# Raw x in tiles of its own, low-rank products in two steps, and the fold in four row groups, in a two-layer attention kernel

## Chip, cores and metric

The kernel runs on one core of one Trainium2 chip. The metric is the device time of one execution in microseconds, as the median of several runs.

## What is computed

The input is an image of 48 x 48 positions with 768 channels, that is 2304 tokens. Two layers follow each other. Each takes its input, normalises it over groups of 24 channels, applies self-attention with 12 heads of 64 channels and relative-position terms, projects, and adds the result to its input. Cut to what matters:

```python
def _gn(v, G=32, eps=1e-5):                 # over all positions and 24 channels
    g = v.reshape(B_, H_, W_, G, C_ // G)
    m = jnp.mean(g, axis=(1, 2, 4), keepdims=True)
    s = jnp.var(g, axis=(1, 2, 4), keepdims=True)
    return ((g - m) / jnp.sqrt(s + eps)).reshape(v.shape)

def _L0_conv_ref(x, qkv_w, qkv_b, FacTu_w, q_facts_w, v_facts_w, FacTv_w, ...):
    qkv = x @ qkv_w + qkv_b
    u = x @ FacTu_w                          # rank 16
    new_q = u @ q_facts_w @ FacTv_w
    new_v = u @ v_facts_w @ FacTv_w
    qkv = qkv.at[..., :C].add(new_q).at[..., 2 * C:].add(new_v)
    ...                                      # q, k, v by heads
    attn = jnp.einsum('bqc,bkc->bqk', q * scale, k)
    attn = ...                               # + rel_h over rows, + rel_w over columns
    out = jax.nn.softmax(attn, axis=-1) @ v
    return out @ proj_w + proj_b

x = x + _L0_conv_ref(_gn(x), ...)
x = x + _L1_conv_ref(_gn(x), ...)            # the same without the low-rank terms
```

The kernel doesn't compute u for every token. It multiplies the three small factors into a 768 x 768 update, and adds this to the weights of Q and V. That addition is the *fold*.

## The kernel before

Tokens are tiled in six blocks (`NQB`) of 384 (`QB`), each with three tiles of 128 (`TPB`); channels are six tiles of 128 (`CT`). Everything works on x transposed, with channels on the partitions: `xT`, one SBUF tile of 128 x 6 x 2304.

**The start of layer 0** is `load_transposed`. SyncE's queue issues six loads of x into tiles `xt` of a pool of their own (L166). Then `weights.begin()` issues the small operands: the low-rank factors `fu` (FacTu), `facts` (the two 16 x 16 factors) and `out` (FacTv, called `fv` in the trace) on ScalarE's queue, the biases and the relative-position tables on SyncE's, and GpSimd (POOL) spreads the tables with L273. `weights.load(0)` and `load(1)` issue the weights of K and Q of the first half of the heads (L299). For each of the 36 pairs of block and channel tile TensorE makes three transposes into a PSUM tile `psx` (L177, three buffers), ScalarE copies it to `xT` (L178), and VectorE takes the statistics from there (L179). After each block, GpSimd's queue stores the raw block to DRAM for the later residual addition (L180, `f_res`). Ahead of block 4 comes `low_rank()`: for each half of the channels three transposes of `fu` (L285), a copy to `fuT` (L286), and for each of the two factors a product (L290, `psl`, 16 rows of result) and a copy to `low` (L293), with two PSUM buffers from the pool `ps_f`.

**The normalisation** (`group_norm`) aggregates the statistics (L187), sums over groups and brings them back to channels with tiny matmuls on TensorE, takes a square root on ScalarE, and returns `normalise(b)`, which rewrites `xT` in place (L226), six operations to a block.

**The projections** (`project`) go through two halves of the heads, and in each through K, Q and V. K and Q come from `head_rows`: 18 PSUM tiles `ps` (pool `ps_mm`, four buffers), each the sum of six matmuls in fp32 (L432), which the hardware's records show as two passes each; VectorE adds the bias (L443), and the result is split into a rounded part (L328, ScalarE) and a difference (L329, VectorE), which GpSimd's queue stores (L369). Q also feeds the relative-position products (L376, `psr`, `psc`). V is 18 tiles `psv` (L461). Before Q and before V, `take` calls `fold`: six matmuls of 16 rows (L320, `psf`, two buffers in `ps_f`), and VectorE adds each into the weights (L324).

**The rest**: attention of six pairs of heads over the stored q, k, v and relative-position products (TensorE under one line, L705), then `out_project` (L874), which also takes the statistics for layer 1, stores its raw input, and leaves `xT` filled.

The order on each engine is a scheduler's, made ahead of time; what is wrapped in `in_order` keeps its place in the program. Each engine takes its instructions in that order, and so does each DMA queue. A second path of the program (`shifted`), which a test on the softmax denominators would start, isn't run with this data.

Of the kernel before, what the change touches and what calls it, by code (L numbers as in the profile page):

```python
# [17 lines left out]
P = 128  # L18
C = 768
# [51 lines left out]
def compute(ctx: ExitStack, tc: tile.TileContext, x, layers, out, run, bad):  # L71
# [72 lines left out]
    if not shifted:  # L144
        places = const.tile([P, 2, P], F32R, tag="places", name="places")
        for i in range(4):
            nc.gpsimd.dma_start(
                places[ts(i, 2 * KG)].bitcast(F32), hot.rearrange("k (u n) -> k u n", u=2)
            )
# [8 lines left out]
    def load_transposed(xT, res, weights):  # L158

        with tc.tile_pool(name="xin", bufs=NQB) as xin, tc.tile_pool(  # L160
            name="ps_x", bufs=3, space=PSUM
        ) as ps_x:
            xts = []
            for b in range(NQB):
                xt = xin.tile([P, TPB, C], F32, tag="xt", name=f"xt_{b}")
                nc.sync.dma_start(xt, x[ts(b, QB), :].rearrange("(j p) c -> p j c", p=P))  # L166
                xts.append(xt)
            weights.begin()
            weights.load(0)
            weights.load(1)  # L170
            for b, xt in enumerate(xts):
                if b == 4:
                    weights.low_rank()
                for t in range(CT):
                    ps = ps_x.tile([P, QB], F32, tag="ps", name=f"psx_{b}_{t}")
                    for j in range(TPB):
                        in_order(nc.tensor.transpose(ps[:, ts(j, P)], xt[:, j, ts(t, P)], ident))  # L177
                    nc.scalar.copy(xT[:, t, ts(b, QB)], ps)  # L178
                    nc.vector.bn_stats(stats[:, t, b, :], xT[:, t, ts(b, QB)])  # L179
                nc.gpsimd.dma_start(res[b], xT[:, :, ts(b, QB)])  # L180

    def group_norm(xT, gn):
# [41 lines left out]
        def normalise(b):  # L224
            for t in range(CT):
                nc.vector.tensor_scalar(  # L226
                    xT[:, t, ts(b, QB)], xT[:, t, ts(b, QB)], mean[:, t : t + 1],
                    rstd[:, t : t + 1], ALU.subtract, ALU.mult,
                )
# [3 lines left out]
    class Weights:  # L233
# [13 lines left out]
        def begin(self):  # L247
            one, ly = self.one, self.ly
            if ly.lora is not None:
                u_w, q_f, v_f, o_w = ly.lora  # L250
                self.fu = one.tile([P, CT, RANK], F32, tag="fu", name="fu")
                nc.scalar.dma_start(self.fu, u_w.rearrange("(t p) r -> p t r", p=P))
                self.facts = one.tile([RANK, 2, RANK], F32, tag="facts", name="facts")
                nc.scalar.dma_start(self.facts[:, 0, :], q_f)
                nc.scalar.dma_start(self.facts[:, 1, :], v_f)
                self.out = one.tile([RANK, C], F32, tag="fv", name="fv")
                nc.scalar.dma_start(self.out, o_w)
            self.bt = one.tile([P, 3 * CT], F32, tag="bt", name="bt")
            nc.sync.dma_start(self.bt, ly.qkv_bt)
            self.vb = one.tile([P, C], F32, tag="vb", name="vb")  # L260
            nc.sync.dma_start(self.vb, ly.v_b.to_broadcast((P, C)))

            self.tables = []
            for a, src in enumerate((ly.relh_t, ly.relw_t)):
                flat = one.tile([P, REL], F32, tag=f"flat{a}", name=f"flat{a}")
                tab = one.tile([P, REL, 2], F32, tag=f"tab{a}", name=f"tab{a}")
                nc.gpsimd.memset(tab, 0.0)
                for par in range(2):  # L270
                    half_rows = ts(par, HD)
                    nc.sync.dma_start(flat[half_rows, :], src)
                    nc.gpsimd.tensor_copy(tab[half_rows, :, par], flat[half_rows, :])  # L273
                self.tables.append(tab.rearrange("p k r -> p (k r)"))
        def low_rank(self):

            if self.ly.lora is None:
                return
            fuT = self.one.tile([RANK, C], F32, tag="fuT", name="fuT")
            self.low = self.one.tile([RANK, 2, C], F32, tag="low", name="low")  # L280
            for half in range(2):
                cols = ts(half, HP * P)
                ps = self.ps.tile([P, HP * P], F32, tag="f", name=f"psu_{half}")[0:RANK]
                for t in range(HP):
                    in_order(nc.tensor.transpose(ps[:, ts(t, P)], self.fu[:, half * HP + t, :], ident))  # L285
                nc.vector.tensor_copy(fuT[:, cols], ps)  # L286
                for i in range(2):
                    ps = self.ps.tile([P, HP * P], F32, tag="f", name=f"psl_{half}_{i}")
                    ps = ps[0:RANK]
                    in_order(nc.tensor.matmul(  # L290
                        ps, lhsT=self.facts[:, i, :], rhs=fuT[:, cols], start=True, stop=True
                    ))
                    nc.vector.tensor_copy(self.low[:, i, cols], ps)  # L293
# [10 lines left out]
        def take(self, mat, half):  # L304
# [5 lines left out]
            if mat != 1:  # L310
                self.fold(w, mat, half)
            return w

        def fold(self, w, mat, half):
# [3 lines left out]
            for t in range(CT):  # L318
                ps = self.ps.tile([P, HP * P], F32, tag="f", name=f"psf_{mat}_{half}_{t}")
                in_order(nc.tensor.matmul(  # L320
                    ps, lhsT=self.low[:, mat // 2, ts(t, P)], rhs=self.out[:, ts(half, HP * P)],
                    start=True, stop=True,
                ))
                nc.vector.tensor_add(w[:, t, :], w[:, t, :], ps)  # L324
# [6 lines left out]
    def project(ly, li, xT, weights, normalise):  # L331
# [17 lines left out]
        with ExitStack() as es:  # L349
            one = es.enter_context(tc.tile_pool(name="p1_one", bufs=1))  # L350
# [53 lines left out]
            def rel_w(half, x):  # L404

                rel = one.tile([2 * HG, HP, N], F32, tag="rel", name=f"relw_{half}")
# [15 lines left out]
            def head_rows(w, half, mat, scale, columns):  # L422

                for b in range(NQB):
# [3 lines left out]
                    for pr in range(HP):  # L428
                        pair = half * HP + pr
                        ps = ps_mm.tile([P, QB], F32, tag="mm", name=f"ps_{mat}_{pair}_{b}")  # L430
                        for t in range(CT):
                            nc.tensor.matmul(  # L432
                                ps, lhsT=w[:, t, ts(pr, P)], rhs=xT[:, t, ts(b, QB)],
# [18 lines left out]
            for half in range(2):  # L452
                head_rows(weights.take(1, half), half, 1, HD**-0.5, None)
                columns = one.tile([P, HP, HG, HG], F32, tag="columns", name=f"columns_{half}")
                head_rows(weights.take(0, half), half, 0, ly.q_scale, columns)
                w_v = weights.take(2, half)
                between = rel_w(half, columns)
                for kt in range(NKT):
                    ps = ps_mm.tile([P, HP * P], F32, tag="mm", name=f"psv_{half}_{kt}")
                    for t in range(CT):  # L460
                        nc.tensor.matmul(  # L461
                            ps, lhsT=xT[:, t, ts(kt, P)], rhs=w_v[:, t, :],
# [383 lines left out]
    def out_project(ly, li, od, early, res, xT, next_res):  # L846
# [3 lines left out]
        with ExitStack() as es:  # L850
# [6 lines left out]
            for b in range(NQB):  # L857
# [11 lines left out]
                else:  # L869
                    y = xT[:, :, ts(b, QB)]  # L870
# [24 lines left out]
    def begin(li, es):  # L895
# [5 lines left out]
        xT = xp.tile([P, CT, N], F32, tag="xT", name=f"xT{li}")  # L901
# [4 lines left out]
    load_transposed(xT, residuals[0], weights)  # L906
    for li, ly in enumerate(layers):
        last = li == len(layers) - 1
        parts = project(ly, li, xT, weights, group_norm(xT, gn))
# [4 lines left out]
        with tc.tile_pool(name="p3_w", bufs=1, **REUSE) as p3:  # L914
# [9 lines left out]
            if not last:  # L924
                xT, gn, weights = begin(1, es)
                weights.begin()
                weights.load(0)
# [60 lines left out]
```

## Time and profile before

The time of three runs was 3400.74, 3394.73 and 3400.97 us, a median of 3400.74.

| | |
|---|---|
| profiled execution, device time | 3399.78 us |
| its span, first to last instruction | 3398.1 us |
| mean granted clock of TensorE in it | 0.992 of full |
| DMA | 406.22 MB, mean 120 GB/s |

By stage, from the busy times in windows (us):

| stage | from | to | PE busy | PEclk | DMA share |
|---|---|---|---|---|---|
| transposes, statistics, normalisation | 0 | 42.05 | 26.92 | 0.84 | 0.98 |
| K, first half | 42.05 | 113.72 | 71.67 | 0.97 | 0.29 |
| Q, with its fold | 113.72 | 204.16 | 90.44 | 0.94 | 0.42 |
| V, with its fold | 204.16 | about 294 | | 1.00 | |
| K, second half | about 294 | 363.80 | | 1.00 | |
| Q, with its fold | 363.80 | 454.20 | 90.40 | 0.94 | 0.42 |
| V, with its fold | 454.20 | 544.17 | 89.27 | 1.00 | 0.58 |
| attention of layer 0 | 544.17 | 1580 | 1033.43 | 1.00 | 0.44 |
| output projection, normalisation | 1580 | 1728.79 | 143.28 | 0.99 | 0.35 |
| layer 1 | 1728.79 | 3398.1 | 1657.19 | 1.00 | 0.42 |

How to read it: PE is TensorE's matmuls, PEld its weight loads, DVE VectorE, ACT ScalarE, POOL GpSimd, SP SyncE. PEclk is the share of its full clock that TensorE was granted. A matmul's record ends where a model puts it, so a busy PE isn't yet a PE at its peak: at half clock it is as busy and does half. Idle time of an engine costs something only where it is on the chain that ends last. `x6` is a count of instructions, and `[3.25 <-PE ps L432]` says that the engine stood idle for 3.25 us before, until that instruction of PE released it.

### The profile page before, as it was taken

What the parts mean: (1) busy time and instruction counts of PE and PEld (TensorE: products, weight loads), DVE (VectorE), ACT (ScalarE), POOL (GpSimd) and SP (SyncE); (2) the same over time, 40 slices, a digit from 0 to 9 for tenths busy, and PEclk for the clock granted to TensorE, in tenths of its full rate; (3) what the DMA queues carried; (4) which work ended last, traced back from release to release, by engine and by line L of the source; (5) the groups of instructions that cost most, each with busy time, mean ns of one, the idle gap of its engine ahead of it and who ended that gap; (6) DMA issues with size and microseconds to landing.
All of it is one profiled execution on the core that took longest, in us unless ns stands there. A gap on an engine that the chain in (4) does not pass through costs nothing.

```text
span 3398.1 us, 49495 instructions
## 1 busy us (share of the span) xinstructions
PE 3361.5 (99%) x19912; PEld 2098.0 (62%) x19912; DVE 1785.3 (53%) x1817; ACT 1246.1 (37%) x1341; POOL 442.7 (13%) x796
## 2 busy tenths in 40 slices
PE   8999999999999999999999999999999999999998
PEld 5565566666666665656556656656666666666665
DVE  5332334666666666665343323366666666666621
ACT  2220223445445454542002203254444444545410
POOL 2111114010101010000001212310202010100000
PEclk8999999999999999999999999999999999999999
DMA  6334339262535353433324424673535352525222
GB/s 242 122 122 136 128 132 243 79 147 64 123 88 119 90 116 94 99 83 127 125 84 139 158 102 157 208 159 84 127 77 131 75 136 70 141 62 107 84 92 109
DMA packets 203486, 406.22 MB, mean 120 GB/s; under 512 B 43264, under 2 KB 83488, under 8 KB 201712
## 3 DMA queue, kind: packets, MB, share of 16 engines
q1 hardware_dynamic: 150816, 239.62, 28.0%
q0 software_dynamic: 51552, 163.23, 14.5%
q8 instruction: 161, 2.64, 0.4%
q14 instruction: 77, 0.63, 0.1%
q10 hardware_dynamic: 880, 0.10, 0.0%
HBM read 253.90 MB, written 148.89 MB: 119 GB/s over the span
## 4 chain that ended last, share of the span: by engine, by line
PE 69%; issue 23%; POOL 3%; DMA 3%; DVE 1%; SPq 0%; ACT 0%; POOLq 0%; DVEq 0%; ACTq 0%
PE ps_sc L705 33%; PE ps_ov L705 25%; PE ps L432 6%; PE psv L461 2%; PE ps_d L705 1%; DMA v<-f_v 1%; DMA f_r<-relw 1%; POOL f_q L369 1%; POOL f_r L402 1%; POOL f_k L369 1%; POOL f_v L467 1%; DMA xt<-in_x_dram 0%; DMA rel<-f_r 0%; PE psr L376 0%; DMA k<-f_k 0%
## 5 line engine op out<-in xcount | busy, mean ns | idle before, releaser
L731 ACT ACTIVATE pt<-ps_sc 128x1024 f32<-128x1024 f32 (+1 forms) x1080 | 1014.3, 941 | 1069.5 <-PE ps_sc L705 991.2
L737 DVE TENSOR_TENSOR sum<-sum,pt 128x1024 f32<-128x1024 f32 (+1 forms) x960 | 1073.9, 1119 | 324.8 <-ACT pt L731 234.5
L705 PE MATMUL ps_sc<-q,k 64*128 64x512 f32 (+1 forms) x8640 | 1093.7, 371 | 0.7 <-DVE v L466 0.7
L705 PEld LDWEIGHTS ps_sc<-q,k 64*128 64x128 f32 x8640 | 804.6, 185 | 217.8 <-issue 129.7
L705 PE MATMUL ps_ov<-pt,v 128*64 128x512 f32 (+1 forms) x4320 | 884.7, 554 | 3.0 <-DMA v<-f_v 1.8
L705 PEld LDWEIGHTS ps_ov<-pt,v 128*64 128x64 f32 x4320 | 294.2, 137 | 498.6 <-issue 462.9
L432 PE MATMUL ps<-xT,w 128*128 128x384 f32 x1728 | 575.7, 493 | 1.6 <-PE bc_rstd L204 1.6
L432 PEld LDWEIGHTS ps<-xT,w 128*128 128x128 f32 x1728 | 329.2, 193 | 227.0 <-issue 10.4
L705 PE MATMUL ps_sc<-rel,places 64*128 64x512 f32 (+1 forms) x2160 | 417.7, 370 | 0.0
L461 PE MATMUL psv<-w,xT 128*128 128x384 f32 x864 | 286.6, 486 | 0.0
L874 PE MATMUL psy<-oT,wproj 128*128 128x384 f32 x864 | 280.9, 486 | 0.0
L766 POOL DMA_DIRECT2D f_rec<-rec x120 | 59.4, 495 | 1638.8 <-DVE rec L758 1625.3
L443 DVE TENSOR_SCALAR x<-ps,bt 128x384 f32<-128x384 f32 x144 | 88.9, 618 | 323.9 <-PE ps L432 323.9
L328 ACT CAST xs<-x 128x1152 fp32r<-128x1152 f32 x48 | 55.3, 1152 | 532.4 <-DVE x L443 532.4
L874 PEld LDWEIGHTS psy<-oT,wproj 128*128 128x128 f32 x864 | 163.2, 190 | 112.1 <-issue 0.8
L705 PEld LDWEIGHTS ps_sc<-rel,places 64*128 64x128 f32 x2160 | 217.6, 185 | 21.0
L758 DVE RECIPROCAL rec<-ps_d 128x512 f32<-128x512 f32 (+1 forms) x60 | 182.2, 3037 | 84.3 <-PE ps_d L705 84.3
L461 PEld LDWEIGHTS psv<-w,xT 128*128 128x128 f32 x864 | 161.1, 190 | 105.0 <-issue 2.2
L737 DVE TENSOR_TENSOR sum<-pt 128x1024 f32<-128x1024 f32 (+1 forms) x60 | 67.1, 1119 | 299.2 <-ACT pt L731 299.2
L655 POOL DMA_DIRECT2D v<-f_v x288 | 148.8, 523 | 202.3 <-PE ps_ov L705 158.4
L466 DVE TENSOR_TENSOR v<-psv,vb 128x384 f32<-128x384 f32 x72 | 39.8, 554 | 152.6 <-PE psv L461 137.7
L329 DVE TENSOR_TENSOR xs<-x,xs 128x1152 fp32r<-128x1152 f32 x48 | 65.1, 1357 | 52.9 <-ACT xs L328 52.9
(90 smaller groups left out, 1087.1 us busy)
## 6 DMA issues: line engine op xcount, KB each, us to landing
rel<-f_r SPq DMA_DIRECT2D x1152, 96.0 KB, 3.9
f_k<-xs POOLq DMA_DIRECT2D x48, 576.0 KB, 3.8
f_q<-xs POOLq DMA_DIRECT2D x48, 576.0 KB, 3.8
k<-f_k SPq DMA_DIRECT2D x72, 384.0 KB, 5.6
q<-f_q SPq DMA_DIRECT2D x96, 256.0 KB, 3.1
f_r<-relh POOLq DMA_DIRECT2D x48, 432.0 KB, 4.2
f_r<-relw POOLq DMA_DIRECT2D x48, 432.0 KB, 6.2
f_res<-xT POOLq DMA_DIRECT2D x12, 1152.0 KB, 10.6
```

The costliest lines, as they stand in the source:

```text
L329: nc.vector.tensor_sub(lo, x, hi.bitcast(F32))
L369: nc.gpsimd.dma_start(to[:, :, ts(b, QB)], part.bitcast(F32))
L432: nc.tensor.matmul(ps, lhsT=w[:, t, ts(pr, P)], rhs=xT[:, t, ts(b, QB)], start=(t == 0), stop=(t == CT - 1),)
L443: nc.vector.tensor_scalar(to, ps, bias, scale, ALU.add, ALU.mult)
L461: nc.tensor.matmul(ps, lhsT=xT[:, t, ts(kt, P)], rhs=w_v[:, t, :], start=(t == 0), stop=(t == CT - 1),)
L655: nc.gpsimd.dma_start(v.rearrange("p (b c) d -> p b c d", c=TPB)[ts(i, KG), :, c], found[i, :, :, c],)
L705: in_order(nc.tensor.matmul(*args, **kwargs))
L731: nc.scalar.activation(pt, ps[:, :, 0 : self.n], AF.Exp)
L737: nc.vector.tensor_add(self.sum, self.first if kt == 1 else self.sum, pt)
L758: nc.vector.reciprocal(self.rec, ps)
L766: nc.gpsimd.dma_start(recs[li][2 * self.pair + r : 2 * self.pair + r + 1, to], self.rec[r * HD : r * HD + 1, :],)
L874: nc.tensor.matmul(ps, lhsT=w[:, t, ts(co, P)], rhs=oT[:, t, :], start=(t == 0), stop=(t == CT - 1),)
```

## The change

- In layer 0, x is loaded straight into `xT`, which is laid out by blocks now (128 x 6 x 6 x 384). The transposed raw values go to six tiles of their own, `raw`, which lie in the buffers that `columns` and `rel` use later; the statistics read them there, and `normalise` reads `raw` and writes `xT`. The pool `p1_one` that holds these buffers is opened ahead of the load for this.
- The stores of the raw blocks come after all blocks and after the tables are spread, in that order on GpSimd's queue. The spreading becomes a step of its own, `spread()`; the loads of `places` are issued after the weights' small operands; K's weights are loaded right behind x.
- `low_rank()` becomes a generator of two steps: the transposes of `fu` ahead of block 2, the products ahead of block 4. Its operands come by GpSimd's queue. `facts` is widened to 128 columns, with the 16 values repeated at columns 0, 32, 64 and 96 and zeros between, so one product leaves its 16 rows four times in `low`, at partitions 0, 32, 64 and 96; FacTv is loaded four times to the same partitions.
- `fold` takes the 16 rows of quarter t % 4 for its matmul t, and its PSUM tiles come from `ps_mm` (four buffers, shared with the projections).

```diff
-    def load_transposed(xT, res, weights):
...
+    def load_transposed(xT, raw, res, weights):
+        with tc.tile_pool(name="ps_x", bufs=3, space=PSUM) as ps_x:
+            loaded = [xT[:, b].rearrange("p t q -> p (t q)") for b in range(NQB)]
+            loaded = [l.rearrange("p (j c) -> p j c", j=TPB) for l in loaded]
             for b in range(NQB):
-                xt = xin.tile([P, TPB, C], F32, tag="xt", name=f"xt_{b}")
-                nc.sync.dma_start(xt, x[ts(b, QB), :].rearrange("(j p) c -> p j c", p=P))
-                xts.append(xt)
+                nc.sync.dma_start(loaded[b], x[ts(b, QB), :].rearrange("(j p) c -> p j c", p=P))
+            weights.load(0)
             weights.begin()
-            weights.load(0)
             weights.load(1)
-            for b, xt in enumerate(xts):
-                if b == 4:
-                    weights.low_rank()
+            if not shifted:
+                load_places()
+            low_rank = weights.low_rank()
+            for b in range(NQB):
+                if b in (2, 4):
+                    next(low_rank, None)
                 for t in range(CT):
                     ps = ps_x.tile([P, QB], F32, tag="ps", name=f"psx_{b}_{t}")
                     for j in range(TPB):
...
-                    nc.scalar.copy(xT[:, t, ts(b, QB)], ps)
-                    nc.vector.bn_stats(stats[:, t, b, :], xT[:, t, ts(b, QB)])
-                nc.gpsimd.dma_start(res[b], xT[:, :, ts(b, QB)])
+                    nc.scalar.copy(raw[b][:, t, :], ps)
+                    nc.vector.bn_stats(stats[:, t, b, :], raw[b][:, t, :])
+            weights.spread()
+            for b in range(NQB):
+                in_order(nc.gpsimd.dma_start(res[b], raw[b]))
...
                 nc.vector.tensor_scalar(
-                    xT[:, t, ts(b, QB)], xT[:, t, ts(b, QB)], mean[:, t : t + 1],
+                    xT[:, b, t, :], raw[b][:, t, :], mean[:, t : t + 1],
                     rstd[:, t : t + 1], ALU.subtract, ALU.mult,
                 )
...
-                nc.scalar.dma_start(self.fu, u_w.rearrange("(t p) r -> p t r", p=P))
-                self.facts = one.tile([RANK, 2, RANK], F32, tag="facts", name="facts")
...
-                self.out = one.tile([RANK, C], F32, tag="fv", name="fv")
-                nc.scalar.dma_start(self.out, o_w)
+                nc.gpsimd.dma_start(self.fu, u_w.rearrange("(t p) r -> p t r", p=P))
+                self.facts = one.tile([RANK, 2, P], F32, tag="facts", name="facts")
+                nc.gpsimd.memset(self.facts, 0.0)
+                self.out = one.tile([P, C], F32, tag="fv", name="fv")
+                for i, f in enumerate((q_f, v_f)):
+                    nc.gpsimd.dma_start(self.facts[:, i, 0:RANK], f)
+                for r in range(4):
+                    nc.gpsimd.dma_start(self.out[r * 32 : r * 32 + RANK, :], o_w)
...
+        def spread(self):
+            for a, (flat, tab) in enumerate(self.tables):
+                for par in range(2):
                     half_rows = ts(par, HD)
-                    nc.sync.dma_start(flat[half_rows, :], src)
-                    nc.gpsimd.tensor_copy(tab[half_rows, :, par], flat[half_rows, :])
...
+                    in_order(nc.gpsimd.tensor_copy(tab[half_rows, :, par], flat[half_rows, :]))
...
         def low_rank(self):
...
-            self.low = self.one.tile([RANK, 2, C], F32, tag="low", name="low")
+            self.low = self.one.tile([P, 2, C], F32, tag="low", name="low")
+            for r in range(1, 4):
+                nc.gpsimd.tensor_copy(
+                    self.facts[:, :, r * 32 : r * 32 + RANK], self.facts[:, :, 0:RANK]
+                )
             for half in range(2):
...
+            yield
+            for half in range(2):
...
-        def fold(self, w, mat, half):
+        def fold(self, w, mat, half, psum):
...
             for t in range(CT):
-                ps = self.ps.tile([P, HP * P], F32, tag="f", name=f"psf_{mat}_{half}_{t}")
+                rows = slice(t % 4 * 32, t % 4 * 32 + RANK)
+                ps = psum.tile([P, HP * P], F32, tag="mm", name=f"psf_{mat}_{half}_{t}")
                 in_order(nc.tensor.matmul(
-                    ps, lhsT=self.low[:, mat // 2, ts(t, P)], rhs=self.out[:, ts(half, HP * P)],
-                    start=True, stop=True,
+                    ps, lhsT=self.low[rows, mat // 2, ts(t, P)],
+                    rhs=self.out[rows, ts(half, HP * P)], start=True, stop=True,
                 ))
                 nc.vector.tensor_add(w[:, t, :], w[:, t, :], ps)
...
-            one = es.enter_context(tc.tile_pool(name="p1_one", bufs=1))
...
-        xT = xp.tile([P, CT, N], F32, tag="xT", name=f"xT{li}")
+        xT = xp.tile([P, NQB, CT, QB], F32, tag="xT", name=f"xT{li}")
...
+        with tc.tile_pool(name="p1_one", bufs=1, **REUSE) as one:
+            raw = [xT[:, b] for b in range(NQB)]
+            if li == 0:
+                raw = [
+                    one.tile([P, NQB // 2, CT, QB], F32, tag=tag, name=f"raw_{tag}")
+                    for tag in ("columns", "rel")
+                ]
+                raw = [raw[b // (NQB // 2)][:, b % (NQB // 2)] for b in range(NQB)]
+                load_transposed(xT, raw, residuals[0], weights)
+            parts = project(ly, li, xT, one, weights, group_norm(xT, raw, gn))
```

Layer 1 keeps its order; its raw blocks are slices of the new `xT`, and its tables are spread by a call of `spread()` behind `begin()`.

## The prediction

> **What bounds the kernel now.** I read the page first: TensorE is never short of work for long, so what counts is where its time is idle or slow.
>
> ```profile
> PE 3361.5 (99%) x19912; PEld 2098.0 (62%) x19912; DVE 1785.3 (53%) x1817; ACT 1246.1 (37%) x1341; POOL 442.7 (13%) x796
> PEclk8999999999999999999999999999999999999999
> ```
>
> 99% leaves 36.6 us idle in the span, and the granted clock is below full only in places. The change touches the start and the four folds of layer 0, so I read those. First the chain of waits over the first 150 us (start, length, what):
>
> ```profile
> 2.36 14.17 DMA xt<-in_x_dram
> ...
> 17.73 2.86 DVE stats L179 x6
> 20.59 0.46 DVE fuT L286
> ...
> 24.47 2.74 PE psl L290 x4
> 27.21 4.69 PE psx L177 x21
> ...
> 32.43 2.90 DVE stats L179 x6
> 35.33 0.76 DVE mv L187 x4
> ...
> 42.05 71.74 PE ps L432 x216
> ```
>
> Until 42.05 nothing is projected. The statistics run on VectorE; between 20.59 and 28.59 it stands mostly behind the low-rank products, a ping-pong with TensorE. Then the granted clock, microsecond by microsecond (columns: window, length, busy time and count of PE, PEld, DVE, ACT, POOL, then PEclk, DMA share, GB/s), in the first Q fold and the first V fold:
>
> ```profile
> 116.00:117.00 1.00, 1.00 (x4) 0.35 (x3) 1.00 (x1) 0.00 (x0) 0.69 (x1) 1.00 0.98 358
> 117.00:118.00 1.00, 1.00 (x3) 0.24 (x2) 0.59 (x2) 0.00 (x0) 0.58 (x1) 0.72 1.06 401
> 118.00:119.00 1.00, 1.00 (x3) 0.50 (x2) 0.55 (x1) 0.00 (x0) 0.15 (x1) 0.50 1.10 424
> 207.00:208.00 1.00, 1.00 (x4) 0.33 (x3) 1.00 (x3) 1.00 (x1) 0.27 (x2) 1.00 1.07 404
> ```
>
> The clock halves 4 us into the Q fold and returns at 127.7; the trace's clock record gives 10.24 us at half. The second Q fold (363.8) does the same, the V folds (204.2, 454.2) do not. Last, VectorE's timeline there:
>
> ```profile
> 113.83 0.62 DVE L443 TENSOR_SCALAR x<-ps,bt 128x384 f32<-128x384 f32 x1 [3.25 <-PE ps L432]
> 114.66 1.20 DVE L324 TENSOR_TENSOR w<-w,psf 128x384 f32<-128x384 f32 x2 [0.22 <-PE psf L320]
> 115.78 1.35 DVE L329 TENSOR_TENSOR xs<-x,xs 128x1152 fp32r<-128x1152 f32 x1
> 117.05 0.55 DVE L324 TENSOR_TENSOR w<-w,psf 128x384 f32<-128x384 f32 x1
> ```
>
> The third addition into the weights ends at 117.60, 3.88 us after K ended at 113.72. That will set the new fold.
>
> **The start.** The six stores of raw x (7.08 MB) go behind all loads, and the low-rank products are split into transposes before block 2 and products before block 4. VectorE's new order is 12 statistics, 2 copies fuT, 12 statistics, 4 copies low, 12 statistics.
>
> Its pace: while ScalarE's copies start 0.64 us apart (7.59, 8.23, ...; TensorE still slow) a tile costs 0.64; of the first 24 (12.49 us) eight cost 5.1, so the other 16 cost 7.4, 0.46 each. Sum: first statistic at 8.1, eight tiles 5.1, 28 tiles 12.9, six copies of 0.55 make 3.3: 29.4. Behind each low-rank step TensorE has to refill the three psx buffers; I charge 0.8 for both. End 30.2 against 35.33.
>
> What must be there: the first x tile was used at 6.65, and 1.18 MB at the 378 GB/s of these rows is 3.1 us, so tile six lands by 22.2 and is used after 27; w for K follows by 25.3 and is used after 36. The tiles of the four weights for the low rank move from ScalarE's queue to POOL's. fu took 9.5 us to land; issued at about 4.8 behind the first hot store it lands near 14.3, just when TensorE reaches psu. The transposes of block 2 are queued behind psu: 0 to 1.5 us, counted in the 0.8. Of POOL's added issues (3 more copies of FacTv among them, 0.5 us each), places (now behind these and still behind hot), three facts copies and the tables, the statistics wait for none; psl needs the facts near 21, and POOL is through places by about 15. The raw stores are last on POOL, behind the tables, and run from about 26 to 45; their only readers to wait are the columns and rel tiles they share space with, first written near 115.
>
> From the last statistic to the first projection took 6.72 us (35.33 to 42.05); it stays. New start 36.9, so **-5.1**. Bounds: -7 (no refill, fu early), -1 (clock falls during the transposes, 24 tiles at 0.64 instead of 0.46).
>
> K then starts at half clock, as before (42.05 to 45.8, 1.9 us lost). The record's changes lie on a grid of 3.413 us whose phase the new start moves; full clock returns one well filled window after the start, on average 4.2 us: 2.1 lost, **+0.2**.
>
> **The four folds.** Old: the 12 passes of psf, between other matmuls, cost 1.49 us for four in the V folds, 4.45 in all. A Q fold adds half of 10.24: 9.6. The gap between K's end and V's fold (90.44) agrees: 216 passes at 0.323 and 80 of psr at 0.13 leave 10.
>
> New: psf draws on the four ps_mm buffers, and the order has six psf, then six projection matmuls, with nothing between. Psf 0 to 2 find buffers free (the third just freed); psf 3 waits for the bias operation of the last K tile, psf 4 and 5 for additions 0 and 1, the first projection matmul for addition 2. Behind it the rest of TensorE waits. VectorE's order stays: bias 0.62, two additions, the difference L329 (which awaits ScalarE's cast), additions. So TensorE resumes when addition 2 ends: **3.85 us per fold**, whatever psf takes.
>
> Here the rule of row packing is weighed. The row: two q·k matmuls of 64 rows overlap (8 in 1.09 us, 386 ns each). The Trainium skill ("TensorE: Matmul & The Clock Gate", Part 3) measured 3.07x for four row tiles; no row here shows four, nor fp32 (12 passes one behind another at 0.37 would take 4.45, a fold 4.5, +2.6 in all). By the rule psf takes 1.5 us instead of 4.45; by the VectorE row TensorE waits anyway. I count 3.85.
>
> The rule that speaks against the change is on the same page of the Trainium skill ("Why this matters for your kernels"): no idle stretch over some 3 us between bursts, or the clock falls. The rows: the window 114.10 to 117.51 had 25% full-array work, the rest psf, and the clock fell; windows in the V fold (202.9 to 209.7) had 38 and 44%, and it stayed. So not idleness decides but a share of full-array work between these; psf of 16 rows counts little. By the rule 3.85 us with psf inside (pauses of 1.3) would keep the clock: four folds at 3.85. By the rows a stretch of 3.85 empties one window below 40% at about 7 phases in 10, in the V folds also, where interleaving had saved it. But the projections behind it are dense, so full clock is back a window or two later: 2.2 to 3.4 us at half fall on them, seldom more. Mean loss 0.7 x 1.7 = 1.2. I take the rows: 5.05 a fold; ends 3.85 and 8.95 (5.1 as before).
>
> Q: 5.05 - 9.6 = -4.55, twice -9.1. V: 5.05 - 4.45 = +0.6, twice **+1.2**.
>
> **Costed at nothing:** x in blocks (each matmul operand remains 384 or 128 adjacent values); normalise from raw to xT (same shape, 474 ns); layer 1's raw stores in longer pieces, under a TensorE-bound projection; attention's first fetches, whose added semaphores belong to raw stores ended 400 us before and whose last wait, VectorE's relw at 520.76, is unchanged. If that cover fails, v at 562.58 is late already (1.21 us) and grows.
>
> **Sum:** -5.1 + 0.2 - 9.1 + 1.2 = -12.8. The profiled execution took 3399.78 (span 3398.1 and 1.7 around it), giving **3387.0**. It lies 1 us under the median 3400.74; one of three runs was at 3394.73, about one lost clock drop (5.1) lower.
>
> **Rivals.**
> - Clock stays full in all folds (packed rows count as work): -5.75 x 2 - 0.6 x 2 - 4.9 = -17.6, **3382.2**. For: four row groups fill what one left empty. Against: psf's work is the same, in less time. 15%.
> - Every fold costs a longer drop (6.8 us at half on dense work, 3.4): Q -2.35 x 2, V +2.8 x 2, start -4.9: -4.0, **3395.8**. 11%. For: 10.24 us drops in both Q folds. Against: at 45.8 and 1732 one dense window sufficed.
> - Folds as forecast, but the start gains nothing because psu stands waiting for fu and the clock falls: -7.9, **3391.9**. 9%. Against: VectorE has the whole of block 0 and 1 ahead of it.
> - The other side: the V folds' stall drops the clock for three windows, as in the old Q folds, in all four: fold 8.95, Q -0.65 x 2, V +4.5 x 2, start -4.9: +2.8, **3402.6**. The change loses from a loss of 4.4 us per fold, 8.8 us of dense work at half. 5%.
> - The forecast, 3383.5 to 3390.5 with serial psf inside it: 60%.
>
> Under 0.2% (6.8 us) this kernel's measurement can't tell a change from none. Faster by more: the forecast, the first rival, most of the third: 0.81. Within: 0.15. Slower: 0.04. Range 3380.5 to 3394.5: it takes in all but the last rival and most of the second.
>
> **What would show it:** first L460 (old L432) matmul at 36 to 38; statistics end near 30; psf in one group, projection resumed 3.8 us after K's end and after the third L353 addition; half-clock stretches of 3.4 or 6.8 us behind some folds, in V too. It is wrong if the first projection stays past 40, if psf delays the additions, or if half clock lasts 10 us.

## The result, and the profile after

The changed kernel took 3391.01 us (median of ten executions, 3388.21 to 3395.84), the kernel before 3400.97 in the same series: ratio 0.9975, 95% interval 0.9967 to 0.9984. In a second series, which is the first experiment below, it was 3391.45 against 3399.01, 0.9978 (0.9969 to 0.9987). By the medians it is 7.6 and 10.0 us faster. Of the 124 executions of the kernel before in the three series below, 22 took only 3386 to 3394 us, at a mean granted clock of 0.995 or 0.996 against 0.990 to 0.994 in all others; all 21 of the changed kernel had 0.992 to 0.994, so against those 22 it gains nothing. The profiled execution happened to be the longest of the ten, 3395.84 with a span of 3394.1; its stages have to be compared one by one, not its end.

From the page of the changed kernel, the busy time of the engines and the granted clock in 40 slices:

```profile
PE 3353.0 (99%) x19912; PEld 2096.5 (62%) x19912; DVE 1784.3 (53%) x1817; ACT 1246.1 (37%) x1341; POOL 443.2 (13%) x807
PEclk9999999999999999999999999999999999999999
```

TensorE is busy for 8.5 us less, with as many instructions. At this grain the clock says nothing more, so I went to the chain of waits of the start (start, length, what):

```profile
2.35 15.20 DMA xT<-in_x_dram
...
18.76 2.86 DVE stats L184 x6
21.62 0.47 DVE low L320
...
22.13 2.88 PE psl L317 x4
25.01 4.05 PE psx L180 x18
...
29.59 3.32 DVE stats L184 x7
32.91 0.75 DVE mv L196 x4
...
39.58 20.48 PE ps L460 x58
```

The first projection starts at 39.58 where it was at 42.05: 2.5 us gained, not 5.1. The low-rank products still stand between two groups of statistics. The folds, in TensorE's timeline (start, length, engine, line, operation; in brackets the idle time before):

```profile
110.94 2.93 PE L349 MATMUL psf<-fv,low 16*128 16x384 f32 x12
114.81 17.20 PE L460 MATMUL ps<-xT,w 128*128 128x384 f32 x48 [0.94 <-DVE w L353]
...
358.29 2.93 PE L349 MATMUL psf<-fv,low 16*128 16x384 f32 x12
362.15 15.75 PE L460 MATMUL ps<-xT,w 128*128 128x384 f32 x48 [0.94 <-DVE w L353]
```

In both, the projection resumes 3.86 us after the one before it ended, released by VectorE. The same 48 matmuls then take 17.20 us in the first and 15.75 in the second: behind the first the clock was at half for a while. VectorE's timeline in the first:

```profile
111.05 0.62 DVE L471 TENSOR_SCALAR x<-ps,bt 128x384 f32<-128x384 f32 x1 [3.25 <-PE ps L460]
111.89 1.02 DVE L353 TENSOR_TENSOR w<-w,psf 128x384 f32<-128x384 f32 x2 [0.22 <-PE psf L349]
112.93 1.36 DVE L358 TENSOR_TENSOR xs<-x,xs 128x1152 fp32r<-128x1152 f32 x1
114.21 1.94 DVE L353 TENSOR_TENSOR w<-w,psf 128x384 f32<-128x384 f32 x4
```

Bias, two additions, the difference, and the third addition, which begins at 114.21 and takes 0.55; it ends where TensorE goes on.

The half-clock stretches of layer 0, from the trace's clock record: behind the first Q fold 3.4 us (10.2 before), behind both V folds 6.8 (none before), behind the second Q fold none (10.2 before).

By stage: start -2.5; from the first projection to attention 502.1 before, 494.9 after, -7.2; from there to the end 2853.9 before and 2859.6 after, +5.7. The last is not the change's: over the fourteen profiles of this study this part took 2851.9 to 2859.6, in no order that follows the edits (the changed kernel's own second profile has 2855.5).

### The profile page after: what moved, and what is told of

Its sections match the earlier page's. It is cut to its first block, busy times and chain, and to the rows that moved or that the text cites. A ratio compares the mean times of both kernels' runs of the same rounds, so it can differ in the third digit from the quotient of the medians.

```text
span 3394.1 us, 49516 instructions
## 1 busy us (share of the span) xinstructions
PE 3353.0 (99%) x19912; PEld 2096.5 (62%) x19912; DVE 1784.3 (53%) x1817; ACT 1246.1 (37%) x1341; POOL 443.2 (13%) x807
## 4 chain that ended last, share of the span: by engine, by line
PE 85%; issue 10%; DMA 2%; POOL 1%; DVE 1%; ACT 0%; SPq 0%; POOLq 0%; ACTq 0%; DVEq 0%
PE ps_sc L733 33%; PE ps_ov L733 25%; PE ps L460 13%; PE psv L489 6%; PE psy L902 4%; PE ps_d L733 1%; PE psr L404 1%; PE psc L404 1%; DMA rel<-f_r 1%; DMA xT<-in_x_dram 0%; DMA v<-f_v 0%; POOL out_dram L920 0%; POOL f_q L397 0%; ACT relw L444 0%; POOL f_r L430 0%
## 5 line engine op out<-in xcount | busy, mean ns | idle before, releaser
L460 PE MATMUL ps<-xT,w 128*128 128x384 f32 x1728 | 570.6, 490 | 3.5 <-DVE w L353 1.9
L460 PEld LDWEIGHTS ps<-xT,w 128*128 128x128 f32 x1728 | 328.1, 192 | 224.8 <-DVE w L353 3.1
L489 PE MATMUL psv<-w,xT 128*128 128x384 f32 x864 | 291.9, 494 | 1.9 <-DVE w L353 1.9
L489 PEld LDWEIGHTS psv<-w,xT 128*128 128x128 f32 x864 | 164.1, 193 | 109.5 <-issue 5.4
```

The lines of the kernel that those rows point to most:

```text
L460: nc.tensor.matmul(ps, lhsT=w[:, t, ts(pr, P)], rhs=xT[:, b, t, :], start=(t == 0), stop=(t == CT - 1),)
L489: nc.tensor.matmul(ps, lhsT=xT[:, kt // TPB, t, ts(kt % TPB, P)], rhs=w_v[:, t, :], start=(t == 0), stop=(t == CT - 1),)
```

## The experiments

To compare folds over kernels whose starts differ, I took the time from the first projection to attention, and subtracted what is left at half clock of K's cold start (half of it, 1.5 to 2.7 us) and 472.1. This last is the same stretch of the spread kernel below without its twelve pairs of psf (12 x 0.84) and its cold start (1.7): 483.95 - 10.1 - 1.7. Its variant with longer pairs gives 472.2, so the base holds to 0.1 us. What remains is the cost of four folds:

| kernel | first projection | from there to attention | four folds | median, us | 95% interval of its ratio to before |
|---|---|---|---|---|---|
| before | 42.05 | 502.1 | 28.2 | 3398.01 to 3400.97 in four series | |
| changed | 39.58 | 494.9 | 21.2 | 3391.01 | 0.9967 to 0.9984 |
| changed, again | 40.15 | 495.6 | 21.6 | 3391.45 | 0.9969 to 0.9987 |
| new start, old fold | 39.91 | 502.0 | 28.2 | 3398.87 | 0.9992 to 1.0012 |
| old start, new fold (first) | 60.01 | 495.2 | 20.4 | 3410.25 | 1.0026 to 1.0054 |
| old start, new fold (second) | 44.91 | 495.1 | 21.3 | 3396.44 | 0.9986 to 1.0003 |
| one row group | 39.84 | 498.7 | 24.8 | 3393.66 | 0.9981 to 0.9995 |
| two psf buffers | 38.23 | 496.7 | 22.9 | 3393.06 | 0.9977 to 0.9992 |
| low rank in one step | 40.97 | 495.5 | 21.5 | 3393.82 | 0.9978 to 0.9992 |
| stores early | 48.97 | 495.5 | 21.5 | 3401.18 | 0.9997 to 1.0017 |
| low rank late | 35.77 | 499.6 | 22.3 | 3391.88 | 0.9971 to 0.9991 |
| spread fold | 38.35 | 484.0 | 10.1 | 3379.06 | 0.9927 to 0.9954 |
| spread fold, one row group | 37.69 | 491.7 | 17.8 | 3387.08 | 0.9956 to 0.9983 |
| spread fold, low rank late | 35.47 | 488.0 | 10.6 | 3382.42 | 0.9933 to 0.9960 |

(For the two with the low rank late, its 3.6 us of passes within K are subtracted too.) Intervals of neighbouring rows overlap where medians lie 2 us apart; there the stages decide, not the medians.

### The changed kernel once more

> The changed kernel once more, beside the same runs of the kernel before as the three below. Theory A (its loss and gain of clock are a matter of phase): layer-0 stages as in its first profile except for the half-clock stretches, which fall on other folds or last other multiples of 3.4 us; TensorE resumes 3.86 us after the projection's end in all four folds; 7 to 10 us under the kernel before. Rival (what its first profile showed is fixed by the code): half clock again 3.4 us in the first Q fold, 6.8 in both V folds, none in the second Q fold.

The stages repeated, but the rival was right about the clock: half clock again 3.4 us in the first Q fold, 6.8 in both V folds, none in the second Q fold. The same four lengths came in three more kernels below (second fold alone, one step, stores early), so in five profiles. Two other kernels with the same fold had other lengths: 3.4 in all four (first fold alone), and 6.8, 3.4, 3.4, 3.4 (low rank late). So the fold's code alone doesn't fix them.

Which windows drop it can be read off. The half-clock stretches begin and end on a grid of 3.41 us. Cut along it (to within 0.1 us), the changed kernel's first profile has, for the full-array work of the projection alone (window, length, TensorE's busy time in L460 and count, PEclk, DMA share, GB/s), and below that for V's matmuls (L489) behind the first V fold:

```profile
110.90:114.30 3.40, 0.11 (x1) 1.00 0.62 180
114.30:117.70 3.40, 2.89 (x5) 0.51 1.05 407
196.20:199.60 3.40, 0.52 (x2) 1.00 0.48 134
356.70:360.10 3.40, 1.66 (x6) 1.00 0.16 26
360.10:363.50 3.40, 1.34 (x4) 1.00 1.02 372
442.00:445.40 3.40, 0.61 (x2) 1.00 0.00 0
```

```profile
199.60:203.00 3.40, 2.49 (x4) 0.51 1.06 410
203.00:206.40 3.40, 3.40 (x6) 0.50 0.38 152
```

Three windows hold 3 to 18% of full-array work, and behind each the clock falls. The second Q fold lies across a boundary of the grid: its stall is cut into windows of 49 and 39%, and the clock stays. The window that follows the first drop is 85% full, and full clock is back after it; behind the V folds it was 73% (2.49 of 3.40), and half clock went on for one window more.

The same count on the exact grid, over layer 0's projections in all fourteen profiles and with the relative-position products taken in (they use all 128 rows too), leaves no exception. At full clock, the 33 windows with at most 32% of such work dropped it, and those with 40% or more kept it; none lies between. At half clock, windows with 85% or more brought full clock back, and those with 81% or less did not. So the lengths follow from where in a window a fold begins: in the five profiles the first Q fold begins 3.0 to 3.4 us after a boundary, in the two others 2.3 and 0.6.

The Trainium skill ("TensorE: Matmul & The Clock Gate", "Why this matters for your kernels") asks for no idle stretch of over some 3 us; TensorE idled 0.94 us in each of the changed kernel's four folds and lost its clock in three.

### The start alone, and the fold alone

The new start with the old fold:

```diff
-                rows = slice(t % 4 * 32, t % 4 * 32 + RANK)
-                ps = psum.tile([P, HP * P], F32, tag="mm", name=f"psf_{mat}_{half}_{t}")
+                rows = slice(0, RANK)
+                ps = self.ps.tile([P, HP * P], F32, tag="f", name=f"psf_{mat}_{half}_{t}")
```

> The changed kernel with the fold put back as it was (two psf buffers of their own, all in the first 16 rows, interleaved with the projection); the new start is kept. Theory A (the start gave 2.5 us, the folds the rest, as the two traces' stage starts say): first projection matmul near 39.6 us into the span, Q folds again with about 10 us of half clock, time 3398 to 3399, 2 to 3 us under the kernel before. Theory B (the start is the gain and the folds only moved within chance): 3390 to 3393. Theory C (forecast's start, 5 us): 3396.

Theory A by the stages: 39.91 at the start, folds at 28.2 as before, 10.2 us of half clock in both Q folds. The time alone can't tell 2 us from nothing. It does exclude theory B: the fold is most of the gain.

The new fold on the kernel before (widened `low` and `facts`, FacTv four times, psf from `ps_mm` in row quarters, one low-rank step ahead of block 4):

> The kernel before with the new fold alone (row quarters, four ps_mm buffers, nothing interleaved); its start is the old one apart from the three further copies of fv and of the facts. Theory A: start at about 42, TensorE resumes 3.85 us after each K and Q projection's end, folds -4.7 and -6 in Q, +2 in V where the clock drops and -0.6 where it doesn't: 3392 to 3396. Theory B: no gain, 3399 to 3402. Theory C (the forecast's folds, -9.1 +1.2): 3393.

The folds did as theory A says (20.4), and the kernel was slower by 12 us. Its chain of waits tells why:

```profile
18.15 18.93 DMA flat<-in_relw_t_dram
...
37.77 0.51 POOL facts L284 x3
38.33 2.92 PE psl L295 x4
```

I had put the three copies that repeat the facts on POOL where the old `low_rank` stands, and there they queue behind the tables' copies, which wait for `flat` until 37. The products wait for the facts, and all transposes behind them: 60.01. With the copies ahead of the tables:

> The kernel before with the new fold alone, built again: the three copies of the facts now stand on POOL ahead of the tables' copies instead of behind them, so psl doesn't wait for flat tables. Theory A: start as in the kernel before, 42 to 43; TensorE resumes 3.86 us after the projections; the four folds together 21 to 22 us instead of 28; time 6 to 7 us under the kernel before. Rival (the fold's gain needs the new start): within 2 us of the kernel before.

Folds 21.3, as in the changed kernel; so their gain, 6.9, doesn't need the new start. But the start went to 44.91, and with 2.9 us given back there the time is within 0.05% of the kernel before. Here the four loads of FacTv and the widened facts are issued by ScalarE, which stands 3.87 us at 8.0 before its next copy of a transposed tile. The parts of the change lean on each other: the fold needs more small operands, and where the old start takes them, they cost 2.9 of the 6.9 us that the fold gains.

### Row quarters and buffers, each alone

All six psf in the first 16 rows, nothing else changed:

```diff
-                rows = slice(t % 4 * 32, t % 4 * 32 + RANK)
+                rows = slice(0, RANK)
```

> The changed kernel with all six psf in the first 16 rows, one behind another; start, buffers and order stay. Theory A (VectorE's third addition sets the stall, the row quarters nearly nothing): psf takes 4.45 us instead of 1.5 to 2.9, the stall 4.5 instead of 3.85, four folds +2.6, time 3392 to 3395, within 0.15% of the changed kernel. Theory B (the row quarters are the gain of the fold): Q folds back to 9.6, 3400 to 3402.

Theory A: psf took 4.1 to 4.5 us in one piece, TensorE resumed with its last pass (4.06 to 4.41 after the projection's end), the folds cost 24.8. By the stages the row quarters are worth 3.4 us in four folds: 1.5 of it stall, most of the rest clock (20.5 us at half in all against 17.1); by the medians 2 to 3.

The row quarters with psf in the two buffers of `ps_f`:

```diff
-                ps = psum.tile([P, HP * P], F32, tag="mm", name=f"psf_{mat}_{half}_{t}")
+                ps = self.ps.tile([P, HP * P], F32, tag="f", name=f"psf_{mat}_{half}_{t}")
```

> The changed kernel with psf in the two buffers of ps_f: row quarters stay, but a psf waits for an addition two back and the scheduler puts projection matmuls between again. Theory A (the four buffers and the undivided group set the clock and the stall): Q folds drop the clock for about 10 us again, V folds do not, time 3396 to 3399. Theory B (row quarters alone save the time): psf's passes no longer fill the gaps, four matmuls of the projection run inside the stall of 3.85, which costs 2.5 plus a clock drop of 1 to 2 windows: 3387 to 3391, no slower than the changed kernel.

Between the theories. The clock went as A has it: 6.8 and 10.2 us of half in the Q folds, none in V. But with shorter passes the interleaved folds cost 22.9 in all. From V's fold through K to the next Q fold took 158.5 here, 159.6 before and 161.6 in the changed kernel: a V fold in the new grouping loses 3 us to row quarters with interleaving.

### What the start is made of

Low rank whole again, ahead of block 4:

```diff
-                if b in (2, 4):
-                    next(low_rank, None)
+                if b == 4:
+                    next(low_rank, None)
+                    next(low_rank, None)
```

> The changed kernel with the low-rank step whole again before block 4 (psu, copies and psl in one), all else as changed. Theory A (splitting it is what the start gained): first projection matmul back at 41.5 to 42.5, time 2 us above the changed kernel. Rival (the stores' place is what it gained): 39.5 to 40.2, no change.

Neither: 40.97, 0.8 to 1.4 later than the changed kernel's two profiles. By these profiles the split is worth about 1 us, but the changed kernel's own two differ by 0.6, so this is no firm figure.

Each store of raw x behind its own block again:

```diff
                     nc.vector.bn_stats(stats[:, t, b, :], raw[b][:, t, :])
-            weights.spread()
-            for b in range(NQB):
-                in_order(nc.gpsimd.dma_start(res[b], raw[b]))
+                in_order(nc.gpsimd.dma_start(res[b], raw[b]))
+            weights.spread()
```

> The changed kernel with each store of raw x issued right behind its block's transposes again, as before, all else as changed. Theory A (the stores took nothing from the loads that mattered): first projection 38 to 40.2, as changed. Rival (7 MB of stores beside the loads delay the last x tiles): the last tiles land 3 us or more later, first projection above 41.5.

The rival, and by more than I gave it. The chain of waits of this kernel, and below it its busy times in the window from 31 (PE, PEld, DVE, ACT, POOL, then PEclk, DMA share, GB/s):

```profile
3.87 32.49 DMA xT<-in_x_dram
...
36.49 4.09 PE psx L180 x18
```

```profile
31.00:36.40 5.40, 0.00 (x0) 0.00 (x0) 0.00 (x0) 0.00 (x0) 0.00 (x0) 0.61 1.03 429
```

All engines stand for 5.4 us while the DMA engines move 429 GB/s: the last tile of x, issued at 3.87, lands 32.5 us later, behind stores. In the changed kernel the same load landed after 20.1 us, at 24.05. The first projection comes at 48.97, and the time is 10 us above the changed kernel. So the stores' place is worth 9 us in the new start. Why did the old start, which also stored early, do without it? POOL's timeline of the kernel before:

```profile
19.91 0.79 POOL L180 DMA_DIRECT2D f_res<-xT  x1 [2.53 <-ACT xT L178]
34.48 0.26 POOL L273 COPY tab<-flat 64x95 f32<-64x95 f32 x1 [13.78 <-DMA flat<-in_relh_t_dram]
...
37.08 1.61 POOL L180 DMA_DIRECT2D f_res<-xT  x2 [0.22 <-issue]
```

Its last two stores stood on POOL behind the tables' copies, which waited for `flat`, until 37.08; and its transposes behind the low-rank step, at 27.21, waited for no x. That the tables' wait was what held the stores back is plain from the rows; that it alone saved the old start I didn't try.

The low-rank step moved out of the start, into K's blocks 1 and 2, folds as changed:

```diff
-                if b in (2, 4):
-                    next(low_rank, None)
...
+                        if li == 0 and half == 0 and mat == 1 and (b, pr) in ((1, 2), (2, 0), (2, 2)):
+                            next(weights.parts, None)
```

> The changed kernel with the whole low-rank step (psu and psl) taken out of the start and put into K's blocks 1 and 2 of half 0; folds as changed. Theory A (the start's missing 2.6 us is the low-rank step: six copies on VectorE, a refill and the clock that it drops): last statistic at 26 to 28 us instead of 32.9, first projection matmul at 33 to 35, K's projection 3.5 to 4.5 longer, time 1 to 2 us under the changed kernel. Rival (the x tiles' landing at 3.8 us each sets the start): first projection stays at 38 to 40, K's projection 3.5 to 4.5 longer, time 3 to 4 above.

First projection at 35.77, 3.8 to 4.4 earlier (not at 33 to 35: the normalisation's small matmuls ran at half clock, from 28.7); the statistics end at 28.4. So the low-rank step is what the start still pays for. But its passes, hidden in the start, stand in the open in K:

```profile
60.63 0.82 PE L306 MATMUL psu<-ident,fu 128*16 128x128 f32 x6
...
65.25 1.55 PE L317 MATMUL psl<-fuT,facts 16*128 16x384 f32 x4
...
74.67 1.55 PE L317 MATMUL psl<-fuT,facts 16*128 16x384 f32 x4
```

3.6 us, and the time is that of the changed kernel. The hoped-for 1 to 2 us are not there.

### A version that beats both

Each fold goes into the projection before it, a pair of psf behind each of the blocks 2, 3 and 4, in the two buffers of `ps_f`, in row quarters; `fold` now takes a pair (t = 2 * pair and 2 * pair + 1) of the weights already loaded:

```diff
-            if mat != 1:
-                self.fold(w, mat, half, psum)
...
+                        if mat < 2 and pr == 2 and 2 <= b < 2 + CT // 2:
+                            weights.fold(1 - mat if mat else 2, half, b - 2)
```

> The changed kernel with each fold spread through the projection before it: after the blocks 2, 3 and 4 of K's rows two psf of Q's fold, likewise V's inside Q's rows, in the two ps_f buffers, in row quarters. Nothing is computed otherwise. Theory A (the fold's cost is VectorE's stall and the clock it drops, not TensorE's passes): no stall, no half clock at the folds, each costs its passes, 6 pairs at 0.4 to 0.9, 2.5 us, against 3.85 to 6.8: 8 to 12 us under the changed kernel. Rival (passes of 16 rows drop the clock wherever they are, or the additions in w delay VectorE's biases): no faster than the changed kernel.

3379.06 us, ratio 0.9927 to 0.9954: 12 us under the changed kernel, 20 under the kernel before. A pair in TensorE's timeline, and VectorE's in the same place:

```profile
75.00 0.92 PE L347 MATMUL psf<-fv,low 16*128 16x384 f32 x4
75.85 11.88 PE L458 MATMUL ps<-xT,w 128*128 128x384 f32 x36
```

```profile
75.11 0.62 DVE L471 TENSOR_SCALAR x<-ps,bt 128x384 f32<-128x384 f32 x1 [3.25 <-PE ps L458]
75.95 1.02 DVE L351 TENSOR_TENSOR w<-w,psf 128x384 f32<-128x384 f32 x2 [0.22 <-PE psf L347]
77.00 1.36 DVE L356 TENSOR_TENSOR xs<-x,xs 128x1152 fp32r<-128x1152 f32 x1
```

TensorE goes on 0.85 us later without a wait, and the additions lie in VectorE's idle time. No half clock at any fold. The base of the table takes the twelve pairs at their passes alone, 10.1; that nothing else is in them is borne out by the old folds, for which the same base gives 28.2 and the rows of the prediction 28.1. VectorE has 3.25 us free before each bias; that was the place for the additions all along.

Here the row quarters can show what they are worth when nothing hides them; all pairs in the first 16 rows:

> The spread fold with all psf in the first 16 rows (no row quarters). Theory A (where VectorE no longer hides TensorE's passes, the row quarters are worth what they save there): a pair takes 1.5 us instead of 0.84, twelve pairs +7.8, time 3386 to 3388 against 3379 for the spread fold. Rival (row quarters are worth nothing here either): 3378 to 3381.

```profile
74.39 1.55 PE L347 MATMUL psf<-fv,low 16*128 16x384 f32 x4
75.87 11.88 PE L458 MATMUL ps<-xT,w 128*128 128x384 f32 x36
```

1.48 for 0.85, twelve times: 7.6 us expected from the rows, 7.7 in the stage, 8.0 in the medians.

And the spread fold with the low rank late:

> Both of the edits above together: low-rank step in K's blocks 1 and 2, Q's fold in K's blocks 3 and 4, V's fold in Q's blocks 2 to 4. Theory A: the sum of the two, 9 to 14 us under the changed kernel. Rival: K's blocks become VectorE-bound (biases, six copies and six additions within three blocks), K's projection grows by more than 8 us and the sum isn't reached.

3382.42: 9.0 under the changed kernel, just what theory A allows, but 3.4 above the spread fold alone, so the late low rank added nothing. K's blocks carry the additions (folds 10.6), and the start came 2.9 earlier at 3.6 of passes. What the profile shows beyond that lies behind the projections, at the first read of v by the attention:

```profile
543.01 5.35 PE L738 MATMUL ps_ov<-pt,v 128*64 128x512 f32 x16 [2.94 <-DMA v<-f_v]
```

TensorE waits 2.94 us for v, and the clock falls for 3.4 us (1.7 lost): together 4.6 us, about what makes the rest of this profile (2859.5) longer than the spread fold's (2855.0). The profile of the low rank late alone has the same drop behind a wait of 2.03; in the other twelve no wait for v there exceeds 1.21, and the clock stays. Why v lands later in these two I didn't try.

## Why the prediction was right, and where it was off

The forecast was 3387.0 with a range to 3394.5, the time 3391.0: faster, by 7.6 to 10 us instead of 13. That is inside the range, but 0.5 us outside the band that the forecast itself claimed (to 3390.5), and nearest to a rival. By stages the start and the folds gave 9.7 and 8.4 us in the two profiles. Two of its signs failed: the first projection was to come at 36 to 38 and the statistics to end near 30, and they came at 39.58 and 32.91. "Wrong if the first projection stays past 40" was missed by 0.4 us in the first profile and met in the second, at 40.15. What follows is the account, point by point:

- **The fold's stall.** Forecast 3.85 us, set by VectorE's third addition whatever psf takes: 3.86 or 3.87 in all 20 folds of the changed order in the five profiles with the same clock pattern. The chain is the one it names: in the first fold psf 3, 4 and 5 and the projection each start 0.05 us after the bias and the additions 0, 1 and 2 end. Row packing itself worked: psf 0 to 2, in three row groups, start within 14 ns and make six passes in 0.92 us (1.9 in one group, at 0.32 a pass); the whole takes 2.93 because of those waits, and four groups side by side no run shows. "Whatever psf takes" went too far: in one row group, with psf at 4.1 to 4.5, the passes set the end, just behind.
- **The old folds.** 9.6 and 4.45, twice each, make 28.1; 28.2 came out of the stage, with the old fold on the new start too.
- **The clock behind the new folds.** Forecast 1.2 us a fold, so 20.2 for four; measured 21.2 and 21.6, or 1.5 a fold. The threshold was right: windows of at most 32% dropped the clock and those of 40% or more did not, where the prediction had 25 against 38 from two folds; and the V folds lost a clock that interleaving had saved. "7 phases in 10" was near as a share (23 of the 28 folds of this order in seven profiles lost the clock) but wrong as a picture: folds that follow each other aren't drawn anew, they share a phase. In the five profiles the first Q fold began 3.4 to 3.8 us ahead of its drop, though their first projections lie between 39.6 and 49.0. K begins at half clock and becomes full at a boundary of the grid, so the work behind it may be tied to the grid there; the first is measured, the second argued.
- **The start.** This term was mis-sized: -5.1 forecast, -2.5 and -1.9 in the changed kernel's two profiles. Up to the end of the 24th statistic the sum came out (21.7 by its working, 21.62 measured), in part by luck: x landed later than 3.1 us a tile (the fourth was there at 17.55, and VectorE waited 0.38), but the first statistic had come 0.33 early. All of the miss lies between there and the last statistic: 11.3 us where I had four copies, twelve statistics and the refill, 8.5. The step that failed is "I charge 0.8 for both". At 22.2 the clock falls to half, just as the second half of the products starts, so psl takes 2.88 for four matmuls that need 1.55; VectorE's third and fourth copy wait for it, and the transposes behind it come at the slow pace until 29:

```profile
23.77 0.56 DVE L320 COPY low<-psl 128x384 f32<-128x384 f32 x1 [1.23 <-PE psl L317]
25.05 0.56 DVE L320 COPY low<-psl 128x384 f32<-128x384 f32 x1 [0.72 <-PE psl L317]
```

I had this as the bound ("clock falls during the transposes") and not as the value, although the kernel before had its clock at half from 21.9 to 32.1.

Where the clock fell later and for one window only, the same start was quicker. The kernel with two buffers, in the chain of waits:

```profile
22.00 1.55 PE psl L317 x4
23.55 4.44 PE psx L180 x24
...
30.94 0.75 DVE mv L196 x4
```

That is 9.5 us instead of 11.3, so at least 1.8 of the 2.8 us missed here go with the clock, and a first projection at 38.23. Seven profiles of this start gave 37.69 to 40.15, so against the one profile before it gains 1.9 to 4.4, never the 5.1. In five of them the normalisation, which I kept at 6.72, took 7.3, at half clock.

- **The late psu of the third rival** (forecast 3391.9, nearest to the measured time) didn't come: psu and its copies were done before the 24th statistic. It had the right time for a wrong reason. The first two rivals fell with the clock record, the last with V folds of 6.8 us at half instead of 10.2.
- **The stores behind all loads** had no term of their own: I took them for harmless behind the loads, and asked no price for the other place. In the new start that price is 9 us. The other edits costed at nothing (x in blocks, layer 1's stores, attention's first fetches) left no mark beyond the spread of 7.7 us in what follows layer 0's projections; v was waited for no longer than 0.77 in the changed kernel's profiles, 1.21 before.

## What to carry to other kernels

Before packing a small matmul more tightly, find what releases the next large one: here it was a vector addition, the packing was worth 3.4 us, and moving the additions to where the vector engine is idle was worth 12. Once that wait was gone, the same packing was worth 8. A step that stops TensorE must be priced with the clock that it loses: cut the trace along the clock's own windows and look at the share of full-array work in each, not at idle time.

## What the hardware showed that was not expected

- The half-clock stretches of the folds had the same lengths in five profiles of four kernels, down to the one fold without any, although these kernels start up to 9 us apart. The Trainium skill ("TensorE: Matmul & The Clock Gate", Part 1) calls the window free-running and its effect variable from run to run. Both are seen here: the changed kernel's two profiles repeat, but two kernels with the same fold at another phase have other lengths. The mean clock of the kernel before ranges from 0.990 to 0.996 over its executions; 0.003 of the span is 10.2 us, as much as its two Q folds lose to the clock in the profile. So it may keep the clock there in some executions; no profile shows one.
- For full clock to return, a window 85% full was enough and one 81% full wasn't, while 40% kept a clock that was still full.
- A load of 1.18 MB, issued at 3.87 us, took 32.5 us to land with stores of the same size on another queue beside it, at 429 GB/s in all; without them the same load took 20.1.
